# A four-layer convolution network on one core: order of the spline layer's first loads, and a pool of its own for the attention layer's `t`

## The chip, the core and the metric

The kernel runs on one NeuronCore of a Trainium2 chip. A core has five engines that run side by side, each through its own list of instructions in a fixed order: TensorE (PE in the profile, its weight loads apart as PEld) multiplies matrices into PSUM, VectorE (DVE) and ScalarE (ACT) work element by element, GpSimd (POOL) does additions and copies here, and SyncE (SP) issues most of the DMA transfers. An instruction waits by semaphores for what it reads and for the buffer that it writes. The metric is the time of one execution on the device in microseconds (us); the median of several runs is compared.

## The reference

The input `x` is (8, 16, 256, 256): eight images of 16 channels. Four layers follow each other, each with a group norm ahead and a residual sum:

```python
x = x + _L0_conv_ref(_gn(x), L0_conv_weights)          # capsule layer, routing in three rounds
x = x + _L1_conv_ref(_gn(x), base, spline, scaler, b)  # spline layer
x = x + _L2_conv_ref(_gn(x), Wq, bq, Wk, bk, Wv, bv)   # attention layer
x = x + _L3_conv_ref(_gn(x), L3_conv_weight)           # circular 3x3 convolution
```

The spline layer is the one that matters most here. For each 3x3 patch it takes a silu and eight cubic B-spline bases of every pixel and sums them with weights; the weights come as (16, 16, 9, 9) and (16, 16, 9, 9, 8) and are first summed over one axis of nine, the spline weights after a product with the scaler:

```python
base_w = base_weight.sum(axis=2)
spl_w = (spline_weight * spline_scaler[..., None]).sum(axis=2)
out = jnp.einsum('bjhwn,ijn->bihw', jax.nn.silu(patches), base_w)
out = out + jnp.einsum('bjhwns,ijns->bihw', bspl, spl_w) + bias
```

The attention layer cuts each channel into 256 patches of 16x16, adds a position embedding, forms Q, K and V with 256x256 matrices, a sigmoid of the scores, and the product with V.

## The kernel before, in words

The four layers run one after the other; what a layer makes goes through scratch tensors in DRAM to the next (`x1` and `x1p` from layer 0 to the spline layer, `x2` to the attention layer, `x3` to the last one).

**The spline layer** (`layer1`) works on 128 strips, 16 for each of 8 images. `features` (L986) fetches a strip's pixels into a buffer `xr` (three buffers; L1002, issued at L994 to L995), and in halves of four row pairs makes from them a distance (ACT, L1012 and L1015), two clipped differences `a` and `e` (DVE, L1023), their squares (ACT, L1029) and cubes (DVE, L1032), the difference of the cubes (POOL, L1041) and a masked copy (DVE, L1044). Both go into one of three rings `bases` that are used in turn; L1049 mends the first and last rows of an image. `silus` (L1063) fetches three small tiles for a strip (`rs` twice, `res`; L1071 to L1073, loads of 256 KB) and takes the silu (ACT, L1082). `conv_strip` multiplies with the weights `tw` and `wm` on PE (L1106), adds bias and residual (DVE, L1143), measures (L1155) and stores (L1158).

Ahead of the first strip, `prepare` (L924) loads the weights: `sw` (1296 KB), `sc` (648 KB) and `main` (1728 KB) into rings 2 and 1, which have no other use yet, and the bias `b1`. DVE multiplies `sw` by `sc` (L937), PE sums both products and `main` over nine terms with the identity (L945, L970) into one PSUM tile, DVE makes `tw` from it (L954 to L966), ACT copies `wm` (L982).

The order of all these instructions is not that of the source. Every piece is handed to a planner (`_Order`, L188) with an engine, a cost in us, a lag until its result can be used, and keys that it reads and writes. The planner walks through a modelled time: it takes the piece that can start first, and among those of its engine within 0.1 us the one with the lowest rank, which is a due time (13.3 us for each set of pieces) less the longest path to the end of the set. What comes out is a fixed list for each engine, SP among them:

```python
op("SP", 0.5, ..., [], [(name,)], lag=16.0 if name == "main" else 10.0)   # L933
op("SP", 0.5, fetch, [], [(xr, 0)], lag=6.0 if i else 13.0)               # L1002
op("SP", 0.5, fetch, [], [(to, 0)], lag=4.0 if i else 16.0)               # L1076
```

The costs and lags thus decide only the order; the chip takes the time that it takes. A set holds the features and silus of one strip and the convolution of the one before. `prepare` is called at the head of set 0 (L1196). `ahead` (L1166) puts five loads for the attention layer (`w_qk`, `w_v`, `w_bqk`, `w_b2v`, `emb0`, 1.28 MB in all) into set 2.

**The attention layer** (`layer2`) goes through 8 images of 16 channels. For each channel `attend` (L1453) makes `t` from the patches (DVE, L1456), adds the embedding (POOL, L1460), and PE then does four products (L1466, L1473, L1481, L1493) with work of DVE and ACT between them. `t` comes from the pool `mid`, which is opened behind the pools `one` and `load`. Tiles of a layer take the place in SBUF of those of the layer before, and the first instruction that writes to such a place waits for what last used it. `w3` (L1350) and the first embeddings and residuals (L1372 to L1377) are fetched at the start.

Of the kernel before, what the change touches and what calls it, by code (L numbers as in the profile page):

```python
# [9 lines left out]
F32 = mybir.dt.float32  # L10
# [7 lines left out]
P = 128  # L18
# [287 lines left out]
class _Net:  # L306
# [544 lines left out]
    def layer1(self, bc, bc4, images=range(B), strips=range(16)):  # L851
# [6 lines left out]
        nc, tc = self.nc, self.tc  # L858
        with ExitStack() as st:
# [3 lines left out]
            wm = one.tile([P, 3, 4, 2 * C], F32, name="wm")  # L863
            sbuf = st.enter_context(tc.tile_pool(name="l1_sb", bufs=1))
            psum = st.enter_context(tc.tile_pool(name="l1_ps", bufs=1, space=PSUM))
            b1 = one.tile([P, 1], F32, name="b1")
# [57 lines left out]
            def prepare(op):  # L924

                at1, at2 = (ring[i].rearrange("p k m w -> p (k m w)") for i in (1, 2))
                sw, sc, main = at2[:, :2592], at2[:, 2592:3888], at1[:, :3456]
                ws = one.tile([P, 2, 3, 3, C], F32, name="ws")
                wf = ws.rearrange("p k h w o -> p (k h w o)")
                ps = buf("sq", [P, 1024])  # L930
                edges(0, op)
                for name, t in (("sw", sw), ("sc", sc), ("main", main), ("b1", b1)):
                    op("SP", 0.5, lambda name=name, t=t: nc.sync.dma_start(out=t, in_=self.d[name]), [], [(name,)], lag=16.0 if name == "main" else 10.0)  # L933

                def scaled():
                    for k in range(2):
                        nc.vector.tensor_tensor(  # L937
                            sw[:, k * 1296 : k * 1296 + 1296], sw[:, k * 1296 : k * 1296 + 1296], sc, ALU.mult
                        )

                def sums():

                    for k in range(2):
                        for m in range(9):
                            nc.tensor.matmul(  # L945
                                ps()[:, k * 144 : k * 144 + 144],
                                self.k["ident"],
                                sw[:, k * 1296 + m * 144 : k * 1296 + m * 144 + 144],
                                start=m == 0,
                                stop=m == 8,  # L950
                            )

                def finish():
                    nc.vector.tensor_copy(wf, ps()[:, :288])  # L954
                    nc.vector.tensor_tensor(wf[:, 144:], wf[:, 144:], wf[:, :144], ALU.subtract)
                    nc.vector.tensor_scalar(wf, wf, 1.0 / 6.0, None, ALU.mult)
                    nc.vector.memset(tw, 0.0)

                    for k in range(2):
                        for q in range(2):  # L960
                            for h in range(2):
                                for ro in range(2):
                                    dh = 2 * q + h - ro
                                    if 0 <= dh < 3:
                                        lanes = slice(64 * h, 64 * h + 64)
                                        nc.vector.tensor_copy(tw[lanes, k, q, :, ro, :], ws[lanes, k, dh])  # L966

                def sums_main():
                    for m in range(9):
                        nc.tensor.matmul(  # L970
                            ps()[:, 512:896],
                            self.k["ident"],
                            main[:, m * 384 : m * 384 + 384],
                            start=m == 0,
                            stop=m == 8,
                        )

                op("DVE", 2.9, scaled, [("sw",), ("sc",)], [("sw",)], mode="shared")
                op("PE", 6.0, sums, [("sw",)], [(ps, 0), ("place", 2)])
                op("DVE", 3.5, finish, [(ps, 0)], [("tw",)], mode="shared")  # L980
                op("PE", 7.0, sums_main, [("main",)], [(ps, 1), ("place", 1)])
                op("ACT", 0.5, lambda: nc.scalar.copy(wm.rearrange("p d n m -> p (d n m)"), ps()[:, 512:896]), [(ps, 1)], [("wm",)])  # L982
                for i in (1, 2):
                    edges(i, op)

            def features(b, j, op):  # L986

                i = b * 16 + j
                t = ring[i % 3]
                pairs = 9 if j == 15 else 8  # L990
                xr = buf("xr", [P, 9 * W])
# [7 lines left out]
                        .to_broadcast([2 * C, 4, pairs * W]),  # L999
                    )  # L1000

                op("SP", 0.5, fetch, [], [(xr, 0)], lag=6.0 if i else 13.0)  # L1002
                for p in range(0, pairs, 4):
                    n = min(4, pairs - p)
                    us = 0.2 + 0.8 * n / 4
# [57 lines left out]
            def silus(b, j, op):  # L1063

                i = b * 16 + j
                res = held[i] = buf("res", [P, 2, W])
                raw = [buf("rs", [P, 2, W]) for _ in range(2)]
                for r, to in ((1, res), (0, raw[0]), (2, raw[1])):

                    def fetch(r=r, to=to):  # L1070
                        nc.sync.dma_start(  # L1071
                            out=to().rearrange("p k w -> p (k w)"),
                            in_=self.x1[j, b, :, r : r + 8].rearrange("c r k w -> r c (k w)"),  # L1073
                        )

                    op("SP", 0.5, fetch, [], [(to, 0)], lag=4.0 if i else 16.0)  # L1076
                for n in range(2):
                    s = sring[i % 2 * 2 + n]
                    key = ("s", i % 2, n)

                    def silu(n=n, s=s):
                        nc.scalar.activation(  # L1082
                            s[:, :, 1 : 1 + W],
                            raw[n](),
                            AF.Silu,
                            bias=bz[:, b : b + 1],
                            scale=bc[:, 1, b : b + 1],
                        )

                    def outside(n=n, s=s):  # L1090
                        row = s[:, n, 1 : 1 + W]
                        nc.vector.tensor_scalar(row, row, keep[:, n : n + 1], None, ALU.mult)

                    op("ACT", 0.8, silu, [(raw[n], 0)], [key])
                    if j == 15 * n:
                        op("DVE", 0.35, outside, [key], [key], mode="shared")
# [69 lines left out]
            def ahead(n, op):  # L1166


                if n == 2:
                    for name, t in self.w2.items():  # L1170
                        op("SP", 0.5, lambda name=name, t=t: nc.sync.dma_start(out=t, in_=self.d[name]), [], [])
                    op("SP", 0.5, lambda: nc.sync.dma_start(out=self.emb0, in_=self.d["emb"][:, :, 0]), [], [])
                if n and n % 16 == 0:
                    b = todo[n - 1][0]

                    def gather():
                        nc.vector.bn_aggr(self.mv2[:, :, b], stats[:, b].rearrange("p n s -> p (n s)"))

                    op("DVE", 0.5, gather, [("st", b, j) for j in strips], [("mv2", b)])
                if n == len(todo) - 16:  # L1180
                    self.bc2, steps = self.stats2_steps(self.small, "g2a", lambda: buf("ps", [P, 512]))
                    reads = [("mv2", b) for b in images]
                    for engine, us, run, banks in steps:
                        op(engine, us, run, reads, [("g2a",)] + [(p, 0) for p in banks])
                        reads = []
                k = n - (len(todo) - 14)
                if 0 <= k < 8 and len(todo) > 32:
                    op("SP", 0.5, lambda: self.patch(images[0], k % 2, k // 2 * 4, 4), [], [])
# [4 lines left out]
            for n in range(len(todo) + 1):  # L1193
                ops = []
                op = lambda *a, **k: ops.append(order.op(*a, **k))
                if not n:  # L1196
                    prepare(op)
                if n < len(todo):
                    features(*todo[n], op)
                if n:  # L1200
                    conv_strip(*todo[n - 1], op)
                if n < len(todo):
                    silus(*todo[n], op)
                ahead(n, op)
                sets.append(ops)
# [154 lines left out]
    def layer2(self, images=range(B), channels=range(C)):  # L1360

        nc, tc = self.nc, self.tc
        images = list(images)
        with ExitStack() as st:
            one = st.enter_context(tc.tile_pool(name="l2_one", bufs=1))
            load = st.enter_context(tc.tile_pool(name="l2_load", bufs=2))
            mid = st.enter_context(tc.tile_pool(name="l2_mid", bufs=2))
# [84 lines left out]

    def attend(self, mid, psum, b, c, pt, res, emb, wqk, wv, bqk, bv, bc, stats):  # L1453
        nc = self.nc
        t = mid.tile([P, 2, 8, 32], F32, name="t")
        nc.vector.tensor_scalar(  # L1456
            t, pt[:, :, c], bc[:, 0, b, c : c + 1], bc[:, 1, b, c : c + 1], ALU.subtract, ALU.mult
        )
# [45 lines left out]
        i = b * C + c  # L1504
# [196 lines left out]
```

## Time and profile before

| | us |
|---|---|
| median of 3 runs (7644.09 to 7649.12) | 7646.63 |
| profiled execution | 7643.24 |
| its span, first to last instruction | 7641.5 |
| spline layer, first convolution to last | 4368.8 to 6132.8 |
| attention layer, first product | 6140.4 |

PE is busy 90% of the span, DVE 71%, POOL 43%, ACT 35%. In the rows of the profile L12 is a line of the kernel; an engine, an operation, the output and input by their names in the program, and a count follow. SPq rows are DMA issues on SP, and their length is that of the issue and not of the transfer. In order of time a row begins with its start and its duration in us, and ends with the idle time of the engine before it and what released it, in brackets. A wait for several semaphores is put down to the one that came last.

### The profile page before, as it was taken

Reading aid. Unit: us, or ns where it says so; the run is one execution under the profiler, and the core shown is the slowest. Engines: PE = TensorE matmul, PEld = TensorE weight load, DVE = VectorE, ACT = ScalarE, POOL = GpSimd, SP = SyncE. Lnnn points to the kernel's source line nnn. Section 1 sums busy time; section 2 is a strip of 40 time slices with the busy share of each in tenths; the row PEclk is TensorE's granted clock in tenths of the full one; section 3 lists DMA queues with packets and bytes.
Section 4 is the critical chain, followed back from the end, with each engine's and each line's share of the span. In section 5 each row is a group of like instructions: output and inputs, shape, how many; then the busy total and the mean of one; then the engine's idle time right before and its main releaser. Section 6 shows DMA issues by size and latency. Waiting matters only on the chain.

```text
span 7641.5 us, 105946 instructions
## 1 busy us (share of the span) xinstructions
PE 6889.0 (90%) x43144; PEld 3276.6 (43%) x43144; DVE 5415.1 (71%) x6462; ACT 2691.9 (35%) x3835; POOL 3248.8 (43%) x1884
## 2 busy tenths in 40 slices
PE   4888888999898999998998499999999999999999
PEld 1333333333333333333333254554545566666634
DVE  5768888887888888888888688888888833333322
ACT  1222222222222222222222277777777712111200
POOL 0545555555555555555555444444444411111100
PEclk9999999999999999999999699999999999999999
DMA  6222222222222222222221344444445533333276
GB/s 243 67 65 76 77 77 77 77 77 77 77 77 77 77 77 77 77 77 76 77 76 50 105 153 156 153 152 152 154 151 161 159 114 97 86 85 97 68 214 189
DMA packets 451065, 813.01 MB, mean 106 GB/s; under 512 B 57490, under 2 KB 299282, under 8 KB 415250
## 3 DMA queue, kind: packets, MB, share of 16 engines
q1 hardware_dynamic: 380946, 738.85, 33.6%
q10 hardware_dynamic: 69632, 67.39, 3.0%
q8 instruction: 340, 5.57, 0.3%
q14 instruction: 147, 1.20, 0.1%
HBM read 595.63 MB, written 211.03 MB: 106 GB/s over the span
## 4 chain that ended last, share of the span: by engine, by line
PE 51%; POOL 21%; DVE 16%; issue 4%; ACT 3%; DMA 3%; SPq 0%; POOLq 0%; DVEq 0%; ACTq 0%
PE ps L1106 13%; POOL dd L765 11%; POOL s L765 8%; PE cv L545 8%; PE pqk L1466 6%; DVE dd L756 4%; PE p3s L1577 4%; PE cv L549 4%; PE pl L654 3%; PE po L1493 3%; PE pv L1473 3%; PE psc L1481 3%; PE fb L622 3%; DMA xr<-x1p 2%; POOL s L810 2%
## 5 line engine op out<-in xcount | busy, mean ns | idle before, releaser
L765 POOL TENSOR_TENSOR dd<-dd 128x1024 f32<-128x1024 f32 x512 | 1206.2, 2356 | 1594.9 <-DVE dd L756 1575.0
L1106 PE MATMUL ps<-bases,tw 128*32 128x512 f32 (+1 forms) x13824 | 1377.8, 550 | 109.6 <-DVE bases L1049 92.0
L756 DVE SCALAR_TENSOR_TENSOR dd<-rb,v 128x1024 f32<-128x1024 f32 (+1 forms) x1024 | 1075.2, 1082 | 206.7 <-PE rb L745 196.8
L554 ACT COPY v<-cv 128x1024 f32<-128x1024 f32 x512 | 518.2, 1012 | 1909.2 <-PE cv L549 1909.2
L1041 POOL TENSOR_TENSOR bases<-e,a 128x1024 f32<-128x1024 f32 (+1 forms) x264 | 744.9, 2823 | 1044.5 <-DVE e L1032 922.0
L545 PE MATMUL cv<-kt,w 128*128 128x512 f32 x2048 | 1090.9, 658 | 38.0 <-DVE dd L756 26.5
L1106 PEld LDWEIGHTS ps<-bases,tw 128*32 128x32 f32 x13824 | 732.4, 109 | 764.9 <-issue 458.3
L644 DVE TENSOR_TENSOR pr<-v,fb 128x2048 f32<-128x2048 f32 (+1 forms) x512 | 1019.5, 2014 | 24.9 <-PE pl L654 20.0
L745 PE MATMUL rb<-rs,ct_fold 32*128 32x512 f32 x3584 | 796.5, 658 | 8.3 <-ACT rs L727 2.7
L765 POOL TENSOR_TENSOR s<-s,dd 128x512 f32<-128x512 f32 x512 | 652.2, 1274 | 29.9
L545 PEld LDWEIGHTS cv<-kt,w 128*128 128x128 f32 x2048 | 366.1, 199 | 598.4 <-issue 389.7
L549 PE MATMUL cv<-kt,w 64*128 64x512 f32 x2048 | 590.9, 654 | 0.0
L654 PE MATMUL pl<-pr,ct_fold 128*32 128x512 f32 x3584 | 525.9, 610 | 61.0 <-DVE pr L644 60.3
L1460 POOL TENSOR_TENSOR t<-t,emb 128x512 f32<-128x512 f32 x128 | 162.1, 1266 | 961.9 <-DVE t L1456 950.8
L622 PEld LDWEIGHTS fb<-f,ct_fold 128*128 128x128 f32 x3072 | 376.7, 195 | 340.7 <-issue 296.7
L622 PE MATMUL fb<-f,ct_fold 128*128 128x128 f32 x3072 | 436.3, 290 | 90.7 <-DVE f L608 88.4
L1466 PE MATMUL pqk<-w_qk,t 128*128 128x512 f32 x1024 | 484.4, 596 | 7.6 <-POOL t L1460 7.6
L765 POOL TENSOR_TENSOR s<-v,dd 128x512 f32<-128x512 f32 x256 | 328.9, 1285 | 319.4 <-DVE dd L756 319.2
L1477 ACT ACTIVATE vt<-pv,w_b2v 128x128 f32<-128x128 f32 x512 | 146.0, 367 | 841.2 <-PE pv L1473 810.8
L1497 DVE TENSOR_TENSOR y<-po,res 128x512 f32<-128x512 f32 x128 | 88.5, 691 | 487.6 <-PE po L1493 487.6
L745 PEld LDWEIGHTS rb<-rs,ct_fold 32*128 32x128 f32 x3584 | 241.2, 188 | 380.7 <-DVE dd L756 211.7
L1032 DVE TENSOR_TENSOR e<-e,sq 128x1024 f32<-128x1024 f32 (+1 forms) x264 | 314.5, 1191 | 95.4 <-ACT sq L1029 95.4
(254 smaller groups left out, 8995.6 us busy)
## 6 DMA issues: line engine op xcount, KB each, us to landing
kt<-d SPq DMA_DIRECT2D x256, 516.0 KB
xr<-x1p SPq DMA_DIRECT2D x120, 1024.0 KB
rs<-x SPq DMA_DIRECT2D x256, 256.0 KB
d<-dn ACTq DMA_DIRECT2D x64, 516.0 KB
xs<-in_x_dram SPq DMA_DIRECT2D x16, 2048.0 KB
xs<-in_x_dram SPq DMA_DIRECT2D x64, 512.0 KB
res<-in_x_dram SPq DMA_DIRECT2D x64, 512.0 KB
x<-s SPq DMA_DIRECT2D x128, 256.0 KB
```

The source lines that it names most:

```text
L545: nc.tensor.matmul(ps()[:, n], w[:, 0, j, :], t[:, a : a + 2, 0:W], start=True, stop=False)
L549: nc.tensor.matmul(ps()[:, n], w[at, 1, j, :], t[at, a : a + 2, 2 - n : 2 - n + W], start=False, stop=True)
L554: nc.scalar.copy(v[h]()[:, 4 * g : 4 * g + 4, j * W : j * W + W], ps().rearrange("p n (a w) -> p (n a) w", w=W),)
L622: nc.tensor.matmul(fb()[:, k * P : k * P + P], unfold[:, h, k, :], f()[:, 3], start=True, stop=True)
L644: nc.vector.tensor_tensor(pr()[:, :n], v[h]()[:, 4 * g : 4 * g + n], p().unsqueeze(1).to_broadcast([P, n, 512]), ALU.mult,)
L654: nc.tensor.matmul(pl()[at : at + 32], sel[:, g, h, :], pr()[:, t, :], start=h == 0 and g == 0, stop=h == 1 and (g == 1 or t == 3),)
L745: nc.tensor.matmul(r()[:, n], spread[at, g, h, :], rs()[at], start=True, stop=True)
L756: nc.vector.scalar_tensor_tensor(dd()[:, :n], r()[:, :n], 1.0 / B, v[h]()[:, a : a + n], ALU.subtract, ALU.mult)
L765: op("POOL", us, lambda: nc.gpsimd.tensor_tensor(out[0](), a[0](), b[0](), ALU.add), a[1] + b[1], out[1])
L1041: nc.gpsimd.tensor_tensor(v, rows(part(e)), rows(part(a)), ALU.subtract)
L1106: nc.tensor.matmul(out if k is None else out[:, k], lhs, rhs, start=start, stop=stop, skip_group_check=True)
L1466: nc.tensor.matmul(ps, t[:, n, k * P : (k + 1) * P], wqk[:, n, :], start=n == 0, stop=n == 1)
```

## The change

Three things change in the spline layer. The loads of the weights get the lengths of their transfers as costs on SP and a lag of 3, the fetches of the first three strips a cost of 2.8, and those of strip 0's small tiles 0.7. `prepare` is called within `features` of strip 0, behind the fetch of `xr`. And the copy of `wm` goes from ACT to DVE. The five loads for the attention layer move from set 2 to set 6. In the attention layer, `t` gets a pool `l2_t` with two buffers, as many as it had, opened ahead of all other pools of that layer.

```diff
@@ spline layer, prepare
+
+                first = dict(sw=3.5, sc=1.8, main=4.6, b1=0.5)
                 for name, t in (("sw", sw), ("sc", sc), ("main", main), ("b1", b1)):
-                    op("SP", 0.5, lambda name=name, t=t: nc.sync.dma_start(out=t, in_=self.d[name]), [], [(name,)], lag=16.0 if name == "main" else 10.0)
+                    op("SP", first[name], lambda name=name, t=t: nc.sync.dma_start(out=t, in_=self.d[name]), [], [(name,)], lag=3.0)
...
-                op("ACT", 0.5, lambda: nc.scalar.copy(wm.rearrange("p d n m -> p (d n m)"), ps()[:, 512:896]), [(ps, 1)], [("wm",)])
+                def finish_main():
+                    nc.vector.tensor_copy(wm.rearrange("p d n m -> p (d n m)"), ps()[:, 512:896])
+
+                op("DVE", 0.5, finish_main, [(ps, 1)], [("wm",)], mode="shared")
@@ features
-                op("SP", 0.5, fetch, [], [(xr, 0)], lag=6.0 if i else 13.0)
+                op("SP", 0.5 if i > 2 else 2.8, fetch, [], [(xr, 0)], lag=6.0 if i else 8.0)
+                if not i:
+                    prepare(op)
@@ silus
-                    op("SP", 0.5, fetch, [], [(to, 0)], lag=4.0 if i else 16.0)
+                    op("SP", 0.5 if i else 0.7, fetch, [], [(to, 0)], lag=4.0)
@@ ahead
-                if n == 2:
+                if n == 6:
                     for name, t in self.w2.items():
...
-                if not n:
-                    prepare(op)
@@ layer2
+            self.tpool = st.enter_context(tc.tile_pool(name="l2_t", bufs=2))
             one = st.enter_context(tc.tile_pool(name="l2_one", bufs=1))
@@ attend
-        t = mid.tile([P, 2, 8, 32], F32, name="t")
+        t = self.tpool.tile([P, 2, 8, 32], F32, name="t")
```

## The prediction

> **What bounds the kernel now.** I read the share of busy time first, then busy time by stage, then the two seams where TensorE (PE) stands still, in order of time. Whole span, and the stages I cut it into (columns of the second: stretch in us, its length, busy us and instructions of PE, PEld, DVE, ACT, POOL, granted clock, DMA share, GB/s):
>
> ```profile
> PE 6889.0 (90%) x43144; PEld 3276.6 (43%) x43144; DVE 5415.1 (71%) x6462; ACT 2691.9 (35%) x3835; POOL 3248.8 (43%) x1884
> ```
>
> ```profile
> 4305.00:4369.00 64.00, 14.49 (x63) 11.55 (x66) 31.14 (x62) 26.00 (x28) 15.02 (x20) 0.58 0.56 178
> 4369.00:4590.00 221.00, 208.66 (x2116) 107.20 (x2112) 185.47 (x216) 158.76 (x162) 90.44 (x32) 0.98 0.48 153
> 4590.00:4811.50 221.50, 209.21 (x2116) 110.42 (x2120) 186.97 (x221) 160.39 (x164) 93.36 (x33) 0.98 0.48 153
> ...
> 6134.00:6141.00 7.00, 0.65 (x1) 0.50 (x2) 2.14 (x5) 0.00 (x0) 1.35 (x1) 0.67 0.41 89
> 6141.00:7277.00 1136.00, 1128.69 (x4138) 771.03 (x4136) 427.56 (x798) 232.08 (x651) 161.37 (x131) 1.00 0.33 92
> ```
>
> Inside the spline layer and the attention layer PE is the bound (209 of 221 us for an image of 16 strips, 1129 of 1136). Before the spline layer's first convolution it works 14.5 of 64 us, and 0.65 of 7 between the layers. The change touches these seams. The first, in order of time:
>
> ```profile
> 4305.97 0.34 SPq L933 DMA_DIRECT2D bases<-in_main_dram  x1
> 4306.36 0.61 SPq L994 DMA_DIRECT2D xr<-x1p  x1
> ...
> 4313.03 2.27 SPq L933 DMA_DIRECT2D b<-in_b_dram  x1
> 4315.34 1.65 SPq L994 DMA_DIRECT2D xr<-x1p  x1
> ...
> 4320.17 2.93 DVE L937 TENSOR_TENSOR bases<-bases 128x1296 f32<-128x1296 f32 x2 [10.12 <-DMA bases<-in_sc_dram]
> ...
> 4329.06 5.97 PE L970 MATMUL sq<-bases,ct_ident 128*128 128x384 f32 x18
> ...
> 4335.06 0.64 SPq L1172 DMA_DIRECT2D emb<-in_emb_dram  x1
> 4335.44 1.28 ACT L1082 ACT_TABLE_LOAD   x1 [29.76 <-DMA w_b2v<-in_b2v_dram]
> ...
> 4339.89 0.69 DVE L1023 TENSOR_SCALAR a<-d 128x1024 f32<-128x1024 f32 x1 [16.79 <-ACT d L1015]
> ...
> 4353.59 0.44 DVE L954 COPY ws<-sq 128x288 f32<-128x288 f32 x1
> ...
> 4368.76 11.95 PE L1106 MATMUL ps<-bases,tw 128*32 128x512 f32 x108 [33.74 <-DVE bases L1049]
> ```
>
> The last row is the start of the convolutions, 33.7 us after PE's sums over the weights. The sums were done at 4335.0, but DVE's L954 came at 4353.6: ahead of it in DVE's fixed order stand features, and they wait for ACT. ACT's first instruction is strip 1's silu, whose `rs` landed only at 4335 (ten loads stand ahead of it; the `w_b2v` that the row names merely ended last). Strip 0's `xr` had lain there since 4315. So the stall is one of order, not of bandwidth.
>
> The second seam:
>
> ```profile
> 6133.73 0.69 DVE L1155 BATCH_NORM_STATS2 st<-y 128x6 f32<-128x512 f32 x1
> ...
> 6138.18 1.00 DVE L1456 TENSOR_SCALAR t<-pt,g2a_bc 128x512 f32<-128x512 f32 x2 [3.03 <-issue]
> 6138.94 1.35 POOL L1460 TENSOR_TENSOR t<-t,emb 128x512 f32<-128x512 f32 x1 [18.43 <-DVE t L1456]
> ...
> 6140.35 6.78 PE L1466 MATMUL pqk<-w_qk,t 128*128 128x512 f32 x8 [7.57 <-POOL t L1460]
> ```
>
> DVE is free at 6135.15 (L1177), but `t` starts 3.03 us later. The program has its first `t` wait for the last store of `y`, issued about 6133.7, since `t` lies where `y` lay.
>
> **The Trainium skill.** "DMA: Bandwidth & Descriptors", Anatomy of one DMA, gives about 2.0 us fixed per DMA plus bytes/436 GB/s. Here `main` (1728 KB) landed 7.0 us after its issue, a little more than its 6.1; a stream of large loads ran at 418 KB/us (below), which agrees. "TensorE: Matmul & The Clock Gate", Part 1, says that an idle window of about 3.4 us halves the clock. The trace agrees: the 8 records of L1466 take 0.85 us each after 7.6 us idle, and 0.43 later. "GPSIMD Engine Reference", Specifications, says that POOL shares its SBUF interfaces with DVE instructions of two SBUF inputs. The trace agrees: L1044 takes 1.28 us as a rule and up to 3.39, two of them 4.63 under POOL's L1041.
>
> **First part: the start of the spline layer.** In the changed program SP issues xr0, sw, sc, main, xr1, rs, rs, res, b1, xr2, ... The first waits for the same stores as before, so 4306. Landings before: the eight DMA semaphores go round, so an issue that waits shows a landing: main 4313.0 (b1's issue), xr0 4315.3, sw 4318.1, sc 4320.1 (L937), rs 4322.7, rs 4325.7, res 4327.6, xr1 4330.0. From 4313.0 to 4320.1, 1024+1296+648 KB in 7.1 us are 418 KB/us. Without `main` ahead of it (1728/418 = 4.1 us) sc lands at 4316.0; xr0, first, at 4306.4 + 2.0 (the page's fixed part, an estimate) + 1024/418 = 2.4, some 4311; main, last of the same four, 4320.1. xr1 is then 2.4 later, 4322.5, the first two rs 4325.2 and 4328.2.
> - ACT no longer waits for silu: 4 instructions on xr0 (2 x 1.22 + 2 x 1.15), 4311 to 4316.
> - DVE: L937 at 4316.0, 2.93 us, to 4319.0; four minima (4 x 0.65) to 4321.6; four cubes, paced by ACT's squares in two buffers, to about 4326.4.
> - PE: first sums as before 1.8 us after sc, 7.1 us, to 4325; `main`'s sums 5.97 to 4331.0. L954 waits for both (one PSUM tile).
> - DVE from 4331.0: L954 to L966 took 5.5 us, 1.8 of them L955 behind POOL, which is then idle: 3.7, to 4334.7. Strip 1's first half: minima 1.3; a square on ACT 1.05 ahead of the first cube, with 0.5 hidden; cubes 2.3: 4338.9. ACT had squares, table load (1.28), two silus (2 x 0.8, second after rs at 4328.2) and strip 1's distances (2.4) done at 4331.4, 3.3 us in time. Then L1044 twice under POOL's sum, 4.63, and the first L1049, 0.4: the first convolution at 4343.9.
>
> Gain 4368.8 - 4343.9 = 24.9 us. Bounds: 21 if the first four loads land together at 4320; 28 if L1044 runs free of POOL (2.6 for 4.6) and sc comes 1 us earlier. I take 24.9.
>
> The `wm` copy moves from ACT (0.47) to DVE; nearest row L954, 288 columns from PSUM in 0.44, so about 0.5 us. It stands behind the two L1049 and PE needs `wm` only after 108 records (10.6 us), so it costs nothing; uncovered it costs 0.5.
>
> **Is the gain kept?** The instruction order of PE is that of before; DVE, ACT and SP differ only in image 0, and images 1 to 7 keep theirs. In image 0 SP's double fetches of xr (two in a row after a gap) move from fetches 11 and 16 to 9 and 14, the places that they have in every later image. Those start, as image 0 now does, with the fetch three strips on just issued (4588.3 for a start at 4589.9; after, 4343 for 4343.9), and take 221.5 us against 221.0. So image 0 should last as long, and the rest shifts.
>
> **The five weight loads** (w_qk to emb0, 1.28 MB) go from set 2 to set 6: now behind strip 5's res and ahead of xr6. Before they cost nothing: rs, which ACT awaited, was ahead. After: SP has a gap there (in image 1 from 4621.4 to the next xr at 4629.8, waiting for DVE), so the issue is covered. The transfers are not wholly: 256 KB loads landed 1.7 to 3.0 us apart, so five are some 11 us, against 8.4 of gap less what still drains. xr6 may land up to 8 us late; xr lands 5.3 us after issue on an empty queue (4368.3 to 4373.6) and ACT takes it about 7 after, so 1.7 of it is slack. What is late next is DVE and POOL. PE is shielded: at a double fetch ACT idles 4.9 us longer (4684.1), and PE in such a stretch loses 0.3 of 12.9. Bounds 0 and 8; I take 1.0.
>
> **Second part: `t` in its own pool** takes the addresses of `tw` and `wm`. DVE's first `t` waits for nothing pending: 6135.15 in place of 6138.18, 3.03 us; POOL and PE follow. The store's wait moves to the first `qk` (PE gives it at 6141, the store landed 6138.2), the second POOL sum (emb, landed 6143.4 as before) and psc. The second sum ends at 6144.8, and PE wants it at 6147.4. Late next would be the first `res`, needed at 6151.9 (before 6154.9): after emb's 768 KB its 2048 KB take 4.9 us, 6148.5. PE idles 4.5 us in place of 7.6, still over 3.4, so cold as before; warm it would gain 2.6 more. The end of the layer and layer 3 keep their waits. Bounds 0 and 5.6; I take 3.0.
>
> **Sum:** 24.9 + 3.0 - 1.0 = 26.9 us. Profiled execution 7643.24 (span 7641.5, 1.7 around it) becomes 7616.3; it lies 3.4 below the median of the runs, 7646.63, which becomes 7619.7.
>
> **Rivals.**
> 1. The weight loads become a new wait: xr6 8 us late, not recovered before the double fetch at 9: gain 20, 7627. For: 1.7 us of slack. Against: ACT is busy 10 of 12.9 us a strip, so recovers 2.9 in each.
> 2. Shorter start: loads sharing 16 engines finish together, sc at 4320: first convolution at 4348, gain 23, 7624. For: the 256 KB loads show how uneven landings are. Against: before, the first four landed in issue order.
> 3. The other side: the head start is owed. Before, PE's start found features of strips 0 and 1 and distances of strip 2; after, those of strip 0 and half of 1. If image 0 pays in PE stalls what DVE lacks (some 5.5 us per half strip, again at each double fetch), three half strips give back 16.5 us, 7636 (no change). From 26.9 us on, image 0 above 248 us, nothing is gained; eight half strips, 44 us, make it slower, 7664. Against: images 1 to 7 start with that little and take 221.5.
>
> **Chances.** Forecast 0.64 (7613 to 7624), rival 1 0.11, rival 2 0.12, more gain than 31 us (clock warm, sums early) 0.05, rival 3 0.08, of which 0.03 slower. A measurement tells about 0.2% (15.3 us) from no change: faster, under 7631, 0.92; same 0.05; slower 0.03. The range 7612 to 7630 holds forecast, rivals 1 and 2.
>
> **What would show it.** First convolution near 4344 and ACT's first distance near 4311; L954 right at the end of `main`'s sums; image 1 at 4566 (not: rival 3, or an ACT wait for xr at strip 6: rival 1); sc at 4320 means rival 2; first L1466 (line moved) 2.4 us after the last L1177. Wrong would be any layer-1 image other than 0 that is not 221 us long.

## The result

The changed kernel takes 7616.64 us in the median of five runs (7613.15 to 7619.93), the kernel before 7645.69 beside it (7640.45 to 7649.12): a ratio of 0.9962, 95% interval 0.9948 to 0.9977, or 29 us. The forecast was 7619.7 us, 26.9 less than before. The profiled execution took 7613.15, its span 7611.4, against 7643.24 and 7641.5.

The changed kernel's shares of busy time are those of before, and so are the stages inside the layers (columns of the second view: stretch in us, length, busy us and instructions of PE, PEld, DVE, ACT, POOL, granted clock, DMA share, GB/s). What is gone is time between the stages: the first line is 39.2 us long where it was 64, the last 4.3 where it was 7.

```profile
PE 6891.6 (91%) x43144; PEld 3281.4 (43%) x43144; DVE 5416.4 (71%) x6463; ACT 2692.1 (35%) x3834; POOL 3248.3 (43%) x1884
```

```profile
4304.40:4343.60 39.20, 14.44 (x58) 11.52 (x58) 25.54 (x57) 24.33 (x25) 11.74 (x19) 0.63 0.73 248
4343.60:4566.00 222.40, 210.60 (x2120) 113.01 (x2124) 188.92 (x224) 160.29 (x164) 93.28 (x33) 0.98 0.51 162
...
6110.30:6114.60 4.30, 0.00 (x0) 0.00 (x0) 3.14 (x7) 0.00 (x0) 1.26 (x1) 1.00 0.31 62
```

The first seam in order of time, changed kernel (start, duration, engine, row; in brackets the idle time before it and what ended it):

```profile
4305.63 0.60 SPq L1001 DMA_DIRECT2D xr<-x1p  x1
...
4311.22 2.37 ACT L1021 ACTIVATE d<-xr,bd,sd 128x1024 f32<-128x1024 f32 x2 [6.21 <-DMA res<-x]
...
4315.72 2.93 DVE L939 TENSOR_TENSOR bases<-bases 128x1296 f32<-128x1296 f32 x2 [5.54 <-DMA bases<-in_sc_dram]
...
4324.80 5.97 PE L972 MATMUL sq<-bases,ct_ident 128*128 128x384 f32 x18
4325.27 1.28 ACT L1091 ACT_TABLE_LOAD   x1 [0.89 <-DMA rs<-x]
...
4330.80 0.46 DVE L956 COPY ws<-sq 128x288 f32<-128x288 f32 x1 [5.17 <-PE sq L972]
...
4338.59 4.58 DVE L1053 SCALAR_TENSOR_TENSOR bases<-xr,xm,bases 128x1024 f32<-128x1024 f32 x2
...
4343.64 8.77 PE L1115 MATMUL ps<-bases,tw 128*32 128x512 f32 x67 [12.88 <-DVE bases L1058]
```

`xr` of strip 0 now goes first, so ACT's first distance stands at 4311 and not behind a silu, at 4337.5. (What it reads is `xr`; the `res` that the row names was issued only at 4309.98.) DVE's copy out of the sums (L956, before L954 at 4353.6) comes when `main`'s sums end and no longer 18.6 us later, and PE waits 12.9 us for the features where it waited 33.7. The second seam, changed kernel:

```profile
6111.21 0.69 DVE L1164 BATCH_NORM_STATS2 st<-y 128x6 f32<-128x512 f32 x1
...
6112.09 0.53 DVE L1186 BATCH_NORM_AGGREGATE mv<-st 128x2 f32<-128x96 f32 x1
6112.54 0.94 DVE L1464 TENSOR_SCALAR t<-pt,g2a_bc 128x512 f32<-128x512 f32 x2
6113.33 1.26 POOL L1468 TENSOR_TENSOR t<-t,emb 128x512 f32<-128x512 f32 x1 [16.05 <-DVE t L1464]
...
6114.65 5.40 PE L1474 MATMUL pqk<-w_qk,t 128*128 128x512 f32 x8 [4.39 <-POOL t L1468]
```

`t` starts as soon as DVE is free; the 3.03 us of idle time ahead of it are gone.

The two profiled spans differ by 30.1 us. Cut at marks that both have: the first layer ended 0.65 us earlier; from its last statistics (L393) to the first convolution 69.52 became 45.05; from there to the last statistics of the spline layer (L1177, now L1186) 1765.9 became 1768.5; from there to the last layer's first product 1142.8 became 1138.2; the last layer took 361.1 in place of 364.0. Only the second and fourth of these belong to the change, as the runs below show.

### The profile page after: what moved, and what is told of

Same layout as the page of the kernel before. It is cut to its first block, busy times and chain, and to the rows that moved or that the text cites. A ratio compares the mean times of both kernels' runs of the same rounds, so it can differ in the third digit from the quotient of the medians.

```text
span 7611.4 us, 105952 instructions
## 1 busy us (share of the span) xinstructions
PE 6891.6 (91%) x43144; PEld 3281.4 (43%) x43144; DVE 5416.4 (71%) x6463; ACT 2692.1 (35%) x3834; POOL 3248.3 (43%) x1884
## 4 chain that ended last, share of the span: by engine, by line
PE 52%; POOL 21%; DVE 16%; issue 4%; ACT 3%; DMA 3%; SPq 0%; POOLq 0%; DVEq 0%; ACTq 0%
PE ps L1115 13%; POOL dd L765 11%; PE cv L545 8%; POOL s L765 8%; PE pqk L1474 6%; PE p3s L1585 4%; DVE dd L756 4%; PE cv L549 4%; PE pl L654 3%; PE po L1501 3%; PE pv L1481 3%; PE psc L1489 3%; PE fb L622 3%; POOL s L810 2%; ACT sq L1038 1%
## 5 line engine op out<-in xcount | busy, mean ns | idle before, releaser
L644 DVE TENSOR_TENSOR pr<-v,fb 128x2048 f32<-128x2048 f32 (+1 forms) x512 | 1020.5, 2017 | 24.9 <-PE pl L654 20.0
```

The source lines that it names most:

```text
L644: nc.vector.tensor_tensor(pr()[:, :n], v[h]()[:, 4 * g : 4 * g + n], p().unsqueeze(1).to_broadcast([P, n, 512]), ALU.mult,)
```

## The experiments

Single times of one kernel lie up to 13 us apart, so the runs are compared by these marks in their traces, one trace for each run. The columns: "start", from L393 to the first convolution; "image 0", from the first convolution to that of image 1; first convolution to the last statistics of the spline layer; from there to the last layer's first product (us).

| kernel | start | image 0 | spline layer | attention layer |
|---|---|---|---|---|
| before | 69.5 | 221.2 | 1765.9 | 1142.8 |
| changed | 45.1 | 220.9 | 1768.5 | 1138.2 |
| e1 loads' costs only | 44.9 | 220.9 | 1767.4 | 1142.3 |
| e2 old costs | 70.3 | 222.0 | 1768.9 | 1139.2 |
| e3 pool of `t` only | 69.8 | 222.4 | 1768.5 | 1138.0 |
| e4 `xr` of strip 0 last | 52.6 | 221.3 | 1765.8 | 1139.3 |
| e5 weight loads four times | 42.9 | 241.1 | 1786.1 | 1138.9 |
| e6 own tile for `main` | 42.1 | 220.5 | 1766.5 | 1139.3 |
| e7 weights finished early | 34.1 | 229.4 | 1774.6 | 1139.2 |
| e8 seam filled | 43.0 | 221.9 | 1769.7 | 1138.4 |
| e9 changed, again | 44.9 | 221.2 | 1768.8 | 1138.3 |
| e10 e6, e8 and a lag | 39.9 | 221.8 | 1767.2 | 1137.1 |
| e11 weight loads twice | 45.0 | 224.8 | 1770.1 | 1139.1 |

### e1: which part makes the start

Before, with nothing but the new costs and lags:

```diff
-  op("SP", 0.5, ..., [(name,)], lag=16.0 if name == "main" else 10.0)
+  op("SP", dict(sw=3.5, sc=1.8, main=4.6, b1=0.5)[name], ..., [(name,)], lag=3.0)
-  op("SP", 0.5, fetch, [], [(xr, 0)], lag=6.0 if i else 13.0)
+  op("SP", 0.5 if i > 2 else 2.8, fetch, [], [(xr, 0)], lag=6.0 if i else 8.0)
-  op("SP", 0.5, fetch, [], [(to, 0)], lag=4.0 if i else 16.0)
+  op("SP", 0.5 if i else 0.7, fetch, [], [(to, 0)], lag=4.0)
```

> The kernel before with only the new costs and lags of the first loads (sw, sc, main, xr of strips 0 to 2, rs and res of strip 0). SP's queue at the start and the start of DVE and ACT then stand as in the changed kernel; the copy of wm stays on ACT, the five weight loads stay at set 2, and t stays in the common pool. Theory (the start is worth the whole of the gain but some 3 to 4.5 us): first convolution 24.5 us earlier than before counted from the end of the first layer, image 0 221 us long, TensorE idle 7.5 us before the attention layer's first product as before, time 24.5 us shorter (ratio 0.9968). Rival (the place of the copy or of the weight loads counts): less than 20 us, or image 0 longer than 224 us.

```profile
4343.59 12.30 PE L1106 MATMUL ps<-bases,tw 128*32 128x512 f32 x108 [12.88 <-DVE bases L1049]
```

Measured: 7616.62 us, ratio 0.9968 (0.9956 to 0.9980), 24.5 us by the medians. Its start is that of the changed kernel, 44.9 us (L393 is at 4298.67), and image 0 lasts 220.9. So the costs and lags alone are worth the whole start; the place of `prepare` in the text, the copy of `wm` on DVE and the move of the weight loads add nothing that can be seen. The three lines were changed together; what each of them is worth isn't separated here.

### e2: the place in the text

The changed kernel with the old costs and lags, `prepare` still behind the fetch of `xr`:

```diff
-  op("SP", first[name], ..., [(name,)], lag=3.0)
+  op("SP", 0.5, ..., [(name,)], lag=16.0 if name == "main" else 10.0)
-  op("SP", 0.5 if i > 2 else 2.8, fetch, [], [(xr, 0)], lag=6.0 if i else 8.0)
+  op("SP", 0.5, fetch, [], [(xr, 0)], lag=6.0 if i else 13.0)
-  op("SP", 0.5 if i else 0.7, fetch, [], [(to, 0)], lag=4.0)
+  op("SP", 0.5, fetch, [], [(to, 0)], lag=4.0 if i else 16.0)
```

> The changed kernel with the old costs and lags of the first loads (0.5 us each; lags 16, 10, 13, 16), while the load of strip 0 still stands ahead of the weights in the program's text. Theory (the planner's due times, not the place in the text, set the order): SP issues main first and ten loads before a load of rs that ACT awaits, the first convolution comes within 4 us of where it was before the change (69.5 us after the last step of the first layer's statistics, against 45.1 changed), time about 22 us above the changed kernel's. Rival (the place in the text does it): the first convolution within 4 us of the changed kernel's.

```profile
4305.50 0.34 SPq L935 DMA_DIRECT2D bases<-in_main_dram  x1
...
4334.33 1.28 ACT L1091 ACT_TABLE_LOAD   x1 [29.18 <-DMA rs<-x]
...
4352.42 0.44 DVE L956 COPY ws<-sq 128x288 f32<-128x288 f32 x1
```

Measured: 7640.5 us (one run), start 70.3. `main` goes first again, ACT waits for `rs` until 4334, and DVE's copy stands behind features at 4352. The order comes from the costs and lags.

### e3: the pool of `t`

The kernel before with the pool alone:

```diff
+  self.tpool = st.enter_context(tc.tile_pool(name="l2_t", bufs=2))
-  t = mid.tile([P, 2, 8, 32], F32, name="t")
+  t = self.tpool.tile([P, 2, 8, 32], F32, name="t")
```

> The kernel before with only t in a pool of its own. Theory: the spline layer's start as before (69.5 us), TensorE idle 4.4 us in place of 7.5 before the attention layer's first product, and the first 8 records of it 5.4 us in place of 6.8, since TensorE comes to its full clock sooner; from the last y of the spline layer to the second channel's first product 13.0 us in place of 17.6, so 4.5 us gained, not 3.0. Rival (3.0 as forecast; the rest was chance): 14.6 us. If the third layer too is some 2.9 us shorter than before the change (364 us), the pool has an effect that the forecast missed; if it is 364 again, that part of the difference was variation.

```profile
6138.55 0.94 DVE L1457 TENSOR_SCALAR t<-pt,g2a_bc 128x512 f32<-128x512 f32 x2
...
6140.66 5.20 PE L1467 MATMUL pqk<-w_qk,t 128*128 128x512 f32 x8 [4.39 <-POOL t L1461]
```

Measured: 7638.92 us (one run). TensorE's gap is 4.39 us as in the changed kernel, the first eight records 5.20, the step from the last `y` to the second channel's first product 12.8 (theory 13.0), and the attention layer 1138.0 us. The last layer is 361.0, and in e1, which has the old code there, 361.5: the 364.0 of the profile before was variation, and none of the change's doing.

The gap is shorter by the same 3.2 us in every run. What TensorE makes of it is not the same: with the pool the first eight records took 5.2 to 5.4 us in three runs and 6.3 to 6.6 in six, without it 6.8 and 6.4. In these six the step from the last `y` is 14.0 to 14.2 us, near the rival's 14.6. Over nine traces with the pool (without the filled ones) the attention layer is 1138.0 to 1139.3, mean 1138.8, against 1142.8 and 1142.3: a gain of 3.7 us, between the 4.5 and the 3.0 of the expectation. By the median times, with 1.3 us or less between e1 and the changed kernel, this part can't be told from nothing: it rests on the traces.

### e4: order of the work against landing of the weights

```diff
-  op("SP", 0.5 if i > 2 else 2.8, fetch, [], [(xr, 0)], lag=6.0 if i else 8.0)
+  op("SP", 0.5 if i > 2 else 2.8, fetch, [], [(xr, 0)], lag=6.0 if i else 0.0)
```

> The changed kernel with the lag of strip 0's load at 0 in place of 8: SP issues sw, sc, main and then xr0 and xr1, and DVE finishes the spline weights ahead of strip 0's features. Theory (the order of the start decides, with the loads as its clock): sc lands 2.4 us earlier (4313.3 for 4315.7), the finishing of the weights starts 2.4 us earlier, at 4328.4, but eight minima and cubes then stand behind it on DVE: first convolution about 5 us later than in the changed kernel, near 4349. Rival (the landing of the weights is what counts): 2.4 us earlier, near 4341.

```profile
4314.81 2.93 DVE L939 TENSOR_TENSOR bases<-bases 128x1296 f32<-128x1296 f32 x2 [3.45 <-DMA bases<-in_sc_dram]
...
4326.98 2.37 ACT L1021 ACTIVATE d<-xr,bd,sd 128x1024 f32<-128x1024 f32 x2 [20.18 <-DMA xr<-x1p]
...
4329.55 0.46 DVE L956 COPY ws<-sq 128x288 f32<-128x288 f32 x1 [11.81 <-PE sq L972]
...
4342.84 2.83 DVE L1032 TENSOR_SCALAR e<-d 128x1024 f32<-128x1024 f32 x1
...
4352.96 3.26 PE L1115 MATMUL ps<-bases,tw 128*32 128x512 f32 x16 [23.44 <-DVE bases L1058]
```

Measured: 7621.45 us (one run). Counted from L393 (4300.36 here, 4298.59 in the changed kernel), the weights are multiplied 2.7 us earlier and their finishing starts 3.0 earlier, but the first convolution comes 7.5 later. The theory said 5, since strip 0's minima and cubes stand behind L956 to L968. For the other 2.5 us the trace shows more than enough: a square stood behind ACT's table load (1.8), and a DVE minimum took 2.83 us in place of 0.69 beside POOL's sum. DVE's order isn't the whole cause either. ACT, which waited for an `xr`, began strip 0 only at 4326.98, so that DVE could have had its first distances at 4330.4 at the earliest; it took them at 4333.3. How much of the 7.5 us is the late `xr` and how much DVE's order isn't separated. What the run does show is that the weights can land earlier and the start come later: their landing isn't what counts.

### e5 and e11: what the weight loads may cost

`xr6` is the load of strip 6's pixels, which now stands behind the five loads. These five at set 6 are made four times (e5) and twice (e11):

```diff
-  for name, t in self.w2.items():
+  for name, t in [*self.w2.items()] * 4:        # e11: * 2, emb0 likewise
```

> The changed kernel with the five weight loads at set 6 made four times over (5.1 MB in place of 1.28 MB ahead of xr6, each into the same tile). Theory (PE is shielded from a late xr6): xr6 is issued some 8 to 11 us later than in the changed kernel (4383.5), ACT waits 5 to 9 us for it (none in the changed kernel), and image 0 is at most 1 us longer than 220.9. Rival 1 of the prediction (what xr6 is late, PE loses): image 0 5 to 9 us longer.

> The changed kernel with the five weight loads at set 6 made twice. From the run with four sets (30.5 us for the four, xr6 issued 23.1 us later than in the changed kernel, image 0 longer by 20.2): one set more is some 7.6 us, of which 2.9 are slack. Theory (a late xr6 costs PE what goes beyond the slack): xr6 issued 5 to 8 us later after the first convolution (39.9 in the changed kernel), image 0 longer by 2 to 5 us, 223 to 226. Rival (PE is shielded up to some point and only the four sets went past it): image 0 within 1 us of 220.9.

With four sets, then with two:

```profile
4403.77 0.55 SPq L1001 DMA_DIRECT2D xr<-x1p  x1
...
4409.24 1.24 ACT L1021 ACTIVATE d<-xr,bd,sd 128x1024 f32<-128x1024 f32 x1 [20.33 <-DMA xr<-x1p]
...
4415.08 5.13 PE L1115 MATMUL ps<-bases,tw 128*32 128x512 f32 x34 [17.07 <-DVE bases L1053]
```

```profile
4389.69 0.61 SPq L1001 DMA_DIRECT2D xr<-x1p  x1
...
4396.35 1.24 ACT L1021 ACTIVATE d<-xr,bd,sd 128x1024 f32<-128x1024 f32 x1 [6.30 <-DMA xr<-x1p]
...
4402.20 7.97 PE L1115 MATMUL ps<-bases,tw 128*32 128x512 f32 x84 [3.03 <-DVE bases L1053]
```

Measured: e5 7630.39 us, e11 7616.22 (one run each). After its first convolution the changed kernel issues xr6 at 39.9 us, e11 at 46.7, e5 at 62.9: 6.8 and 23.1 later, 6.8 and 7.7 us for each set more. (A repeated load waits for the one before it into the same tile: in e5 SP waits 8.0 us for `w_qk` and 8.2 for `emb`.) Image 0 is longer by 4.0 and 20.2. The expectation of e5 falls: PE isn't shielded. The difference is 2.9 us in both, the slack, and e11 came out as its own expectation had it. That the two agree to 0.1 us is in part chance: in e11 nearly all of the 4.0 is waiting, in e5 PE waits 17.4 us more than in the changed kernel, and its work takes 2.8 us longer, part of it behind the long wait, with a granted clock of 0.50 until 4418. So beyond some 3 us of slack a late xr6 costs PE about its lateness. One set, as in the change, stays inside: xr6 goes out 39.9 us after the start of image 0, as its counterpart did in image 1 before the change (4629.8 after 4589.9), and ACT waits for none.

### e6: the wait for `main`'s sums

```diff
+  pm = buf("ps", [P, 512])
-  ps()[:, 512:896],          # sums of main, and the copy of wm
+  pm()[:, :384],
```

> The changed kernel with the sums over main in a PSUM tile of their own, so that DVE's finishing of the spline weights waits for the first sums alone. Theory: the copy that begins the finishing starts when DVE's four cubes are done (4325.6, in place of 4330.8 at the end of main's sums), is over at 4329.3, and then ACT bounds: minima at 4330.6, squares at 4332.9, first convolution near 4341.2, 2.4 us earlier and not 5.2. Rival (the wait for main's sums is on the path in full): 5.2 us earlier, 4338.4.

```profile
4326.23 5.97 PE L973 MATMUL ps<-bases,ct_ident 128*128 128x384 f32 x18
4326.84 0.45 DVE L957 COPY ws<-sq 128x288 f32<-128x288 f32 x1
4327.64 2.36 POOL L1051 TENSOR_TENSOR bases<-e,a 128x1024 f32<-128x1024 f32 x1
4327.67 2.50 DVE L959 TENSOR_SCALAR ws<-ws 128x288 f32<-128x288 f32 x1
```

Measured: 7611.74 us (one run), start 42.1, 3.0 us earlier than in the changed kernel's first trace and 0.8 earlier than in the quickest of the six with its order (42.9 to 45.1); image 0 keeps it. Its first sums took 7.56 us, as long as in the runs that start at 44.9 to 45.1 (see the end), so 3.0 compares like with like. The copy runs beside `main`'s sums as the theory had it, but what then bounds is DVE and not ACT: L959 takes 2.50 us beside POOL's sum, 0.31 alone. So the size came out near the expected 2.4 for another reason, which is luck, and the rival's 5.2 is out.

### e7: is a head start owed?

On top of e6, lags that pull the finishing and strip 0's last steps ahead of strip 1's features:

```diff
-  op("DVE", 3.5, finish, [(ps, 0)], [("tw",)], mode="shared")
+  op("DVE", 3.5, finish, [(ps, 0)], [("tw",)], mode="shared", lag=4.0)
   # right and outside of strip 0: lag=4.0 and lag=6.0
```

> The kernel of the run before (own PSUM tile for main's sums), with lags in the planner that put the finishing of the spline weights and strip 0's last steps ahead of strip 1's first features on DVE. The first convolution comes near 4333, 10 to 11 us earlier than in the changed kernel, but with nothing of strip 1 ready. Theory (a head start is owed only as far as DVE can't catch up: it has 12.1 of 12.9 us of work a strip): PE waits 3 to 6 us in image 0, and image 1 starts 5 to 8 us earlier than in the changed kernel. Rival 3 of the prediction (the head start is owed in full): image 1 starts within 1 us of the changed kernel's, image 0 230 us long or more.

```profile
4333.05 7.91 PE L1116 MATMUL ps<-bases,tw 128*32 128x512 f32 x56 [2.21 <-DVE bases L1059]
4343.04 6.20 PE L1116 MATMUL ps<-bases,tw 128*32 128x256 f32 x50 [2.08 <-POOL bases L1051]
4356.75 7.97 PE L1116 MATMUL ps<-bases,tw 128*32 128x512 f32 x84 [1.93 <-DVE bases L1054]
4397.69 7.97 PE L1116 MATMUL ps<-bases,tw 128*32 128x512 f32 x84 [1.86 <-DVE bases L1054]
```

Measured: 7610.2 us (one run). The start is 11.0 us earlier than the changed kernel's, and image 0 8.5 longer (229.4): image 1 begins only 2.4 earlier (263.5 us after L393 for 265.9), where 5 to 8 were expected. Within image 0 PE stands 8.0 us for features, 2.1 in the changed kernel. Most of the other 2.6 is clock: after the wait of 2.08 us the granted clock was 0.76, 0.50 and 0.89 in the three stretches of 2 us from 4343 on, 10 us after the start, where the changed kernel has 1.00. That makes 1.7 us (an estimate from these shares); the rest isn't settled. Neither expectation holds, but rival 3's mechanism exists: what PE starts ahead of the first half of strip 1 is mostly owed. e6, which starts 8 us later with that half ready, reaches image 1 at 262.6, no later than e7.

### e8: the clock in the second seam

Three products ahead of the first, into a PSUM tile that nothing reads:

```diff
+  if b == 0 and c == 0:
+      ps = psum.tile([P, 512], F32, name="pqk")
+      for n in range(3):
+          nc.tensor.matmul(ps, wqk[:, 0, :P], wqk[:, 0, :], start=n == 0, stop=n == 2)
```

> The changed kernel with three added products of w_qk by itself (into a PSUM tile that nothing reads) ahead of the attention layer's first product, while TensorE would stand idle. Theory (the idle time costs clock): with less than 3 us of idle time left the first product's 8 records take 3.4 us in place of 5.2 to 6.8, and from the start of DVE's last statistics of the spline layer to its second qk it is 6.0 to 6.5 us, against 7.8 to 9.2 with t's own pool and 12.1 to 12.6 without: 2 us gained. Rival (the slow first product is a wait for its operands): 7.8 us or more.

```profile
6111.32 2.81 PE L1470 MATMUL pqk<-w_qk 128*128 128x512 f32 x6 [1.17 <-DVE y L1152]
...
6114.54 3.70 PE L1478 MATMUL pqk<-w_qk,t 128*128 128x512 f32 x8 [0.40 <-POOL t L1472]
...
6121.94 2.48 POOL L1472 TENSOR_TENSOR t<-t,emb 128x512 f32<-128x512 f32 x2 [7.45 <-DMA emb<-in_emb_dram]
6123.25 2.84 PE L1478 MATMUL pqk<-w_qk,t 128*128 128x512 f32 x6 [1.55 <-POOL t L1472]
```

Measured: 7613.51 us (one run). With 1.17 and 0.40 us of idle time left the eight records take 3.70 us, and the step from the last statistics to the second `qk` 6.30, as the theory had it. The granted clock shows the cause: 0.55 and 0.59 from 6115 to 6119 in the changed kernel, 1.00 here. So the slow product is a cost of the idle time. But the gain is taken back at once: the second channel's `t` waits for `emb` until 6121.9, and the first product of that channel stands 11.27 us after the last statistics, in the changed kernel 11.25. What is late next is that load.

### e9 and e10: the changed kernel beside all three

e9 is the changed kernel; e10 adds to it the own tile of e6, the filling of e8 and a lag that puts strip 0's `right` (L1053) ahead of the finishing of the weights:

```diff
-  op("DVE", 1.27 * us, right, ..., mode="shared")
+  op("DVE", 1.27 * us, right, ..., mode="shared", lag=0.0 if i else 4.0)
```

> The changed kernel once more, unaltered, beside the next. The first convolution 43 to 45 us after the start of the first layer's last statistics (the five runs of this order so far gave 45.1, 44.9, 42.9, 43.0, the difference being the moment at which TensorE's sums come to full clock), image 0 within 1 us of 220.9, and the third layer 361 to 362 us. Time 24 to 30 us below the kernel before (ratio 0.9962 to 0.9968).

> The changed kernel with the own PSUM tile for main's sums, a lag that puts DVE's last multiplications of strip 0 (bases) ahead of the finishing of the weights, and the three filling products before the attention layer. As the features of strip 1's first half are still ready when the convolutions begin, nothing should be owed. Theory: first convolution near 39.5 us after the start of the last statistics (42.1 with the own tile alone), image 0 within 1 us of 220.9, the step from the last statistics to the second qk 6.3 us; 6 to 8 us below the changed kernel (ratio to the kernel before near 0.9955). Rival (what the run with the weights finished early showed: an earlier start is owed): image 0 longer than 223 us and image 1 no earlier than 262 us after that start.

```profile
4334.68 1.31 DVE L1054 SCALAR_TENSOR_TENSOR bases<-xr,xm,bases 128x1024 f32<-128x1024 f32 x1 [2.52 <-POOL bases L1051]
4337.15 0.44 DVE L957 COPY ws<-sq 128x288 f32<-128x288 f32 x1
4343.14 2.80 DVE L1059 TENSOR_SCALAR bases<-bases,ct_ident,lost 128x256 f32<-128x256 f32 x2
4343.70 6.60 PE L1116 MATMUL ps<-bases,tw 128*32 128x512 f32 x36 [7.83 <-DVE bases L1059]
```

Measured on one chip: e9 7615.30 us (7613.21 to 7619.07), ratio 0.9967 (0.9954 to 0.9979); e10 7610.32 (7607.56 to 7612.62), ratio 0.9959 (0.9946 to 0.9973). e10 is 5.0 us below e9, and their runs don't overlap. Its first layer ended 5.1 us later in the profile (L393 at 4303.81 against 4298.70); from there the convolutions start at 39.9 us, 5.0 earlier than in e9, image 0 lasts 221.8 (image 1 at 261.7), and up to the last layer it is 7.8 us shorter. By the medians the gain is short of the 6 to 8 us expected, by the traces it isn't. With half of strip 1 ready, nothing is owed that shows above the variation of image 0 (220.9 to 221.9).

## Why the prediction was right, point by point

**The start, -24.9.** Three traces with the old order have 69.5 to 70.3 us, six with the new one 42.9 to 45.1; the two profiled before and after differ by 24.5, the means by 25.6. The steps hold to within 0.4 us: ACT's first distance 4311.2 (forecast 4311), `sc` 4315.7 (4316.0), the copy 4330.8 (4331.0), the last cube's end 4338.7 (4338.9), first convolution 4343.6 (4343.9), though the first layer had ended 0.65 earlier here; counted from there they come that much later, and the gain is 24.5. The forecast took all four loads at the stream's rate in issue order; that rival 2 would have them land together at 4320 is answered by the same row. The 2.0 us that it put ahead of `xr` are given by the Trainium skill, "DMA: Bandwidth & Descriptors", Anatomy of one DMA, for DMAs that GpSimd issues, and these are issued by SP; here `xr` was in use 5.6 us after its issue, where the sum had 4.4, and an issue 0.8 us earlier than forecast (4305.6 for 4306.4) hid the difference. That the stall was one of order was then tried from both sides: e1 moves the same bytes in another order and has the whole gain, e2 takes it away again. e4 excludes the landing of the weights.

**Is it kept?** Yes: image 1 starts at 4564.5 (forecast 4566) and image 0 lasts 220.9 us, in all runs with this start and no other edit to image 0's loads 220.9 to 221.9. Rival 3 fails here, but not because image 0 owes nothing whatever it starts with: e7 gives back 8.5 of 11.0 us. The prediction looked at images 1 to 7, which start with as little; it is half a strip of features that makes the difference (e7 against e6 and e10). Its last sign of being wrong was too strict: image 6 takes 224.5 to 226.1 us in every trace, 225.5 before the change too, and only images 1 to 5 lie at 220.0 to 222.9.

**The weight loads, +1.0.** Measured: nothing. The bound of 8 us was too wide for one set, and the reason given for a small value, that PE is shielded from a late xr6, is wrong: e5 and e11 show some 3 us of slack and then about the full price. xr6 was simply not late. That 1.0 was near the truth is luck. Rival 1 had the mechanism right and the size wrong.

**`t`, -3.0.** The gap shrank by 3.2, forecast 3.0; the attention layer by 3.7 over all traces, as the first product is also shorter, 6.1 us in the mean for 6.6. "Cold as before" was right that the shorter gap still costs clock: in e8, filled, the product gains 1.5 to 2.9 us. Named late next was the first `res`; what is late next in e8 is `emb`.

**The sum.** 25.6 + 3.7 makes 29.3 us by the traces; the two sets of medians gave 29.05 and 26.6. Forecast: 26.9. The differences of the terms (0.7, 0.7 and 1.0) lie inside what single runs vary by.

## What to carry to other kernels

When a planner lays out the queues, a wrong cost or lag for a load is a wrong order of everything behind it: give the first loads the times that their transfers take, and see what the first instruction of each engine waits for. In this kernel, how far ahead the engine that bounds may start is decided by the features that are ready one step on, not by its first operands; past that point an earlier start is lent, not given. Find the slack of a moved load by making it twice.

## What the runs showed of the hardware

A DVE instruction with one tensor input can be held for the whole of a POOL sum: L959 took 2.50 us beside POOL's 2.36 (e6; alone 0.31), L1032 2.83 beside 2.72 (e4; alone 0.69), the pair L1059 2.80 beside 2.48 (e10; alone 0.72). The Trainium skill, "GPSIMD Engine Reference", Key points, names as contending the DVE instructions "with two SBUF inputs" and those in a 2-port mode. These have one tensor input, so if the page covers them it is by the mode, which no run here tells.

After the same 4.39 us of idle time the first eight records took between 5.20 and 6.60 us. The first sums at the start of the spline layer took 6.13 and 6.20 us in the two runs that start at 42.9 and 43.0, and 7.42 to 7.55 in the four that start at 44.9 to 45.1: that is most of the spread of the start. The Trainium skill, "TensorE: Matmul & The Clock Gate", Part 1, says that the window which decides the clock is free-running, so that the moment differs from run to run; the traces agree. How long TensorE stood still doesn't decide alone: after 2.08 us in e7 the granted clock fell to 0.50, after 3.03 us in e11 it stayed at 1.00. So the idle time of 3.4 us by which the prediction called the product cold is no safe limit.
